# A second norm's scale and shift moved to where a tile is turned, and the last units' way reordered

## The chip, the cores and the metric

The kernel runs on one core of a Trainium2 chip. The metric is the device time of one execution in microseconds. The profile is of one execution, by the hardware profiler. Its engines are TensorE (PE, with its weight loads PEld), VectorE (DVE), ScalarE (ACT), GpSimd (POOL) and SyncE (SP), which issues most DMAs here.

## The reference

Two layers run over x of shape (4, 1024, 256): batch 4, 1024 positions, 256 channels.

```python
x = x + attn(_layernorm(x))          # causal, 16 heads of 16, alibi bias, projection w_proj
x = x + ffn(_layernorm(x))
```

The second one reads its input as T=4, B=1024, C=256, so its own attention is over the four batch rows at each of the 1024 positions, and has then a mixture of experts:

```python
h = _layernorm(x + attn_out, ln1_g, ln1_b)      # scale and shift: gain g, shift b
logits = flat @ router_w.T + router_b           # flat = h.reshape(-1, C)
_, top_i = jax.lax.top_k(softmax(logits), 2)
assign = jnp.max(top_i, axis=-1)                # one expert of 8 for each of 4096 tokens
he = gelu(flat @ w1[e].T + b1[e], approximate=False)
oe = he @ w2[e].T + b2[e]                       # for the assigned expert only
return _layernorm(h + moe_out, ln2_g, ln2_b)    # h is the residual
```

## The kernel before

All work is issued in an order written by the program itself: the kernel's Python simulates the engines' clocks with rough costs and emits each piece where that clock says it is due. What is emitted is fixed; on the chip each engine runs its instructions in that order and waits by semaphores.

**Attention.** Queries are split into units (`units`): a chunk of 256 positions of one batch row; the last chunk's are halves of 128, so that eight small units end the stage. For each unit, TensorE makes scores (tiles `sk`), ScalarE exponentials (`p`), POOL masks the diagonal blocks, TensorE weighs the values (`pv`), and `yt` takes the result. For all but the last unit it goes to DRAM (`y`), comes back in another layout with its sums (`sums`, `yc`), the reciprocals of the sums go out (`r`) and come back broadcast (`su`), VectorE divides (`yc` by `su`), TensorE projects with `wp` (tile `op`) and VectorE adds to x. These are `load_sums`, `invert`, `load_inverse`, `divide` and `projected`, put in due lists by `attended` (L2165), at times after the unit's end named `SUMS_BY`, `INVERTED_BY`, `Y_BY`, `DIVIDED_BY` and `PROJECTED_BY`. The last unit is divided on chip: `normalise` takes sums on TensorE (`sum`), a reciprocal and a product on VectorE (`yn`), and `project_slots` projects it.

**Fronts.** `front(i)` (L1577) does everything of a block of 128 positions x 4 batch rows up to the routing: statistics and root (the root runs on POOL, L814), `u` normalised, turned on TensorE (`utp`, `ut`), products for q, k and v (`qkvp`, copied to `qkv` and `vr`), the small attention over four rows on VectorE (`pr`, `sc`, then `pv`, `ctx`), turned again (`ctp`, `ct`), output product (`ao`), the sum in `u`, the norm (`stats_h`, `rstd_h`), the key, the rank and the one-hot choice (`hot`), then `u` times G1 plus B1, and the place of each token within its expert (`place`). `u` and x (with B2 already added) are stored to DRAM as the two halves of `rows`, through SP's queue. Of the eight fronts, six run beside attention. Fronts 6 and 7 end in the tail; for them ScalarE applies the norms. Each `yield` hands over to the planner, with a kind and a cost.

**Tables and tiles.** Tokens are sorted by expert into tiles of 128. Table 0 has 18 tiles with the tokens of the first six fronts; table 1 has the other 20 and can be made only when front 7's tokens are placed (`who` on TensorE, then some VectorE instructions that end in `rows`, `at_t`, `at_w`). Per tile: POOL gathers the rows (`given`, an indirect DMA, L1849), TensorE turns them (`mtp`), ScalarE copies that (`mt`), TensorE makes `hid` with w1, ScalarE the gelu (`ge`), and TensorE `oe` with w2. The residual is added by a product with the identity (`by_product`: table 0 and the last two tiles), otherwise by VectorE into `given`. Two tiles at a time are finished: statistics, root on POOL (`rstd_v`), two VectorE instructions per tile for the output `o`, and an indirect DMA of POOL that scatters it (L1965), after a small memset (L1964). The queue has 18 buffers for gathered rows and four for `o`.

**The tail** begins after the last attention unit (L2302 on): what is still due, the last unit's division and projection, then a loop that chooses between the steps of fronts 6 and 7, of the tables and of tiles by its own clocks (`free`, `W1_THERE`, `threads[0].ready`).

Of the kernel before, what the change touches and what calls it, by code (L numbers as in the profile page):

```python
# [29 lines left out]
F32 = mybir.dt.float32  # L30
# [7 lines left out]
P = 128  # L38
# [5 lines left out]
CC = C // P  # L44
# [23 lines left out]
HELD_BACK = 5  # L68

TILE = (("PE", 2.6), ("DVE", 1.7), ("ACT", 1.9), ("POOL", 2.3))  # L70
TILE_HALF, LAG, COPIED, FIRST_BY, W1_THERE, LOAD_W2 = 1.3, 0.2, 1.0, 0.1, 22.0, 10.0
KQ_BUFS = 2
D_SLOT = 10.0
SWITCH, COLUMN, EXP_AT_ALL, EXP, READ = 0.2, 1 / 600, 0.17, 1 / 1200, 0.7
AHEAD, EARLY_BY, ROOT, OF_D = 1.0, 0.2, 1.4, 0.35
SUMS_BY, INVERTED_BY, Y_BY, DIVIDED_BY, PROJECTED_BY = 7.0, 14.0, 16.5, 26.0, 28.0

EXP_ZERO = -126 * math.log(2.0)

# [526 lines left out]
def fast_layer(ctx: ExitStack, tc: tile.TileContext, odd, x, wq, wk, wv, wp, w_in, w_out, w_r,  # L606
# [119 lines left out]
    def wide(a):  # L726
        return a.unsqueeze(1).to_broadcast([P, B] + list(a.shape)[1:])
# [130 lines left out]
    def store(key, what):  # L858
        stores.append([key, 0, what])
# [717 lines left out]
    def front(i, fact, more, last):  # L1577
# [14 lines left out]
        def for_later(t):  # L1592

            nc.vector.tensor_tensor(at_x(t), at_x(t), row(B2), ALU.add)
# [21 lines left out]

        yield "D", 2.4
        ut = flipped(u, "ut")
        yield "E", 1.7
        for t in range(B):  # L1620
            for_later(t)
        store(("x", i), store_later)
        yield "DQ" if more else "D", 2.8
        qk = fact.tile([P, B, QC], F32, tag="qkv", name=f"qkv_{i}")
        vr = fact.tile([P, B, C + E], F32, tag="vr", name=f"vr_{i}", bufs=2)
# [74 lines left out]
        if last:  # L1700

            ct = fact.tile(
                [P, CC, QC], F32, tag="turned", name=f"ct_{i}", bufs=TURNED if more else 2
            )

            def turned_sum(t, pr):
                pt = bank(f"ctp_{i}_{t}")[:, :C].rearrange("p (c q) -> p c q", q=P)
                for cc in range(CC):
                    for k in range(B // 2):
                        nc.tensor.matmul(  # L1710
                            pt[:, cc], pr[:, k, cc * P:(cc + 1) * P], ident,
                            start=k == 0, stop=k == B // 2 - 1,
                        )
                nc.scalar.copy(ct[:, :, t * P:(t + 1) * P], pt)

            pr = None
            for t in range(B):
                yield "E", 2.0, 1.0 if t else 0.0
                if t:
                    turned_sum(t - 1, pr)  # L1720
                pr = weighted(t)
                nc.vector.tensor_tensor(pr[:, 0:2], pr[:, 0:2], pr[:, 2:4], ALU.add)
            yield "D", 1.0
            turned_sum(B - 1, pr)
        else:
            ctx_ = fact.tile([P, B, C], F32, tag="ctx", name=f"ctx_{i}")
            for t in range(B):
                yield "E", 2.3
                pr = weighted(t)
                nc.vector.tensor_tensor(pr[:, 0:2], pr[:, 0:2], pr[:, 2:4], ALU.add)  # L1730
                nc.vector.tensor_tensor(ctx_[:, t], pr[:, 0], pr[:, 1], ALU.add)
# [28 lines left out]
        if last:  # L1760
# [4 lines left out]
        norm_apply(  # L1765
            lambda t: u[:, t], lambda t: u[:, t], B, mv, rstd, f"h_{i}", scalar=i >= NT - 2
        )
        key = small.tile([P, B, E], F32, tag="key", name=f"key_{i}", bufs=2)
        best = small.tile([P, B], F32, tag="best", name=f"best_{i}", bufs=2)
        each_e = lambda a: a.unsqueeze(2).to_broadcast([P, B, E])  # L1770
# [27 lines left out]
        nc.vector.tensor_reduce(best, rank, AX.X, ALU.max)  # L1798
        hot = small.tile([P, B, E], BF16, tag="hot", name=f"hot_{i}", bufs=2)
        nc.vector.tensor_tensor(hot, iota, each_e(best), ALU.is_equal)  # L1800
        yield "E", 2.2
        nc.vector.tensor_tensor(u, u, wide(row(G1)), ALU.mult)
        nc.vector.tensor_tensor(u, u, wide(row(B1)), ALU.add)
        store(("u", i), lambda: nc.sync.dma_start(rows_of[:, :, 0:C], u))
        yield ("DC" if last else "D"), 0.8

        if last:
# [31 lines left out]
    class Tile:  # L1839
# [46 lines left out]
        def stages(self):  # L1886


            work, ps, j, name = late["work"], late["ps"], self.j, self.name
            pt = ps.tile([P, CC, P], F32, tag="t", name=f"mtp_{name}")  # L1890
            for cc in range(CC):
                nc.tensor.transpose(pt[:, cc], self.hx[:, cc * P:(cc + 1) * P], ident)
            mt = work.tile([P, CC, P], F32, tag="mt", name=f"mt_{name}")
            nc.scalar.copy(mt, pt)
            if not self.w1:
                self.copy_w1()
            yield
            if not self.w2:
                at = nc.values_load(
                    self.table.at_w[0:1, j:j + 1], engines=[mybir.EngineType.PE],  # L1900
                    min_val=0, max_val=(E - 2) * CC * C,
                    skip_runtime_bounds_check_because="an expert is 1 to E - 1",
                )
            sel = self.table.chosen[:, j:j + 1].to_broadcast([P, P])
            ph = ps.tile([P, CC, P], F32, tag="h", name=f"hid_{name}")
            for fc in range(CC):
                for cc in range(CC):
                    nc.tensor.matmul(
                        ph[:, fc], self.w1[:, cc, fc * P:(fc + 1) * P], mt[:, cc],
                        start=cc == 0, stop=False,  # L1910
                    )
                nc.tensor.matmul(
                    ph[:, fc], b_bf[0][:, fc * P:(fc + 1) * P], sel, start=False, stop=True
                )
            late["n_hid"] += 1
            ge = work.tile([P, CC, P], F32, tag="ge", name=f"ge_{name}")
            nc.scalar.activation(ge, ph, AF.Gelu)
            yield
            if late["n_oe"] % 2 == 0:
                if late["wide"] and late["n_oe"] % 4:  # L1920
                    late["oe"] = bank(f"oe_{name}").rearrange("p (k c) -> p k c", c=C)
                else:
                    late["oe"] = ps.tile([P, 2, C], F32, tag="o", name=f"oe_{name}", bufs=3)
            self.v = late["oe"][:, late["n_oe"] % 2]
            late["n_oe"] += 1
            for fc in range(CC):
                nc.tensor.matmul(
                    self.v, ge[:, fc],
                    self.w2[:, fc] if self.w2 else late["w2"][:, bass.ds(at + fc * C, C)],
                    start=fc == 0, stop=False,  # L1930
                )


            if self.by_product:
                nc.tensor.matmul(self.v, ident, self.hx[:, :C], start=False, stop=False)
            nc.tensor.matmul(self.v, sel, b_bf[1], start=False, stop=True)

    def finish_tiles(two):

        n, name = len(two), two[0].name  # L1940
        for t in two:
            if not t.by_product:
                own = t.hx[:, :C]
                nc.vector.tensor_tensor(own, own, t.v, ALU.add)
                t.v = own
        mv, rstd = norm_stats(lambda k: two[k].v, n, f"v_{name}", "_v")
        norm_root(rstd, n)
        yield
# [26 lines left out]
    class Experts:  # L1975
# [8 lines left out]
        def fetch(self):  # L1984
            self.step += 1
            if tiles_to_do and self.n_fetched - self.n_finished < len(given):
                t = tiles_to_do.pop(0)
                t.by_product = t.table.n == 0 or len(tiles_to_do) < 2
                t.gather(given[self.n_fetched % len(given)])
                if self.n_fetched < N_OWN:  # L1990
                    t.load_weights()
                self.n_fetched += 1
                self.fetched.append((t, self.step))
# [171 lines left out]
    def attended(u, at):  # L2165
        size = units[u][2]
        if u == last_unit:
            return
        for by, what, cost in (
            (SUMS_BY, load_sums, 0.0), (INVERTED_BY, invert, 0.3), (Y_BY, load_inverse, 0.0),  # L2170
            (DIVIDED_BY, divide, 0.5),
        ):
            due_E.append((at + by, cost, lambda what=what: what(u)))
        due_D.append((at + PROJECTED_BY, 0.9 * size, lambda: projected(u)))

    n_projected = [0] * NT

# [111 lines left out]
    for p in range(len(rounds) // 2):  # L2289
# [9 lines left out]
            del waiting[:2]  # L2299
        fill()  # L2300
        E_slot(2 * p + 1, then)
    weigh_next(waiting)  # L2302
    issue_stores(age=0)
    attention.close()
    half_of.clear()
    tail_banks.append(ctx.enter_context(pool("ps_m", 3, space=PSUM)))


    assert not of_E and not of_D, (sorted(of_E), sorted(of_D))
    for _, what in pop_due(due_E + [], 1e9):  # L2310
        what()
    for g in range(2, G):
        normalise(g)
    for _, what in pop_due(due_D + [], 1e9):
        what()
    for it in running:
        it.ready = 0.0
    load_sums(last_unit)
    project_slots()
    tail = ctx.enter_context(pool("tail", 1))  # L2320
    work = ctx.enter_context(pool("work", 2))
    ps_x = ctx.enter_context(pool("ps_x", 1, space=PSUM))
# [46 lines left out]


    threads = [Running(front(NT - 1, fact, 1, True))] + running + [Running(prepare_rest())]
    free = {"PE": 8.0, "DVE": 6.0, "ACT": 2.0, "POOL": 6.0}
    threads[0].ready = 9.0
    engine_of = {"E": "DVE", "P": "DVE", "A": "ACT", "N": "ACT", "R": "POOL", "D": "PE", "d": "PE"}

    def begin(it):
# [149 lines left out]
```

## Time and profile before

| what | value |
|---|---|
| time, median of 3 runs | 809.62 us (807.39 to 810.99) |
| the profiled execution's own time | 812.74 us |
| its span, first to last instruction | 811.0 us |
| granted TensorE clock, mean | 0.958 |
| PE busy | 711.0 us, 88% |
| DVE busy | 544.4 us, 67% |
| ACT busy | 415.7 us, 51% |
| POOL busy | 256.0 us, 32% |
| exponentials of the attention (ACT, `p<-sk`) | 320 instructions, 287.2 us |
| gathers (POOL, L1849) | 38, 42.6 us |
| scatters (POOL, L1965) | 38, 39.7 us |

Busy time is the sum of instructions' durations. An engine can be busy little and yet never rest, since the time between two DMA issues of POOL isn't counted. In the rows of a timeline the columns are start, duration, engine, line, operation, tiles (output before input), shapes and count; the bracket holds the idle time before it and what ended it. Line 587 is the helper that issues every TensorE, VectorE and ScalarE instruction, so these are told apart by their tiles.

### The profile page before, as it was taken

Reading aid. Unit: us, or ns where it says so; the run is one execution under the profiler, and the core shown is the slowest. Engines: PE = TensorE matmul, PEld = TensorE weight load, DVE = VectorE, ACT = ScalarE, POOL = GpSimd, SP = SyncE. Lnnn points to the kernel's source line nnn. Section 1 sums busy time; section 2 is a strip of 40 time slices with the busy share of each in tenths; the row PEclk is TensorE's granted clock in tenths of the full one; section 3 lists DMA queues with packets and bytes.
Section 4 is the critical chain, followed back from the end, with each engine's and each line's share of the span. In section 5 each row is a group of like instructions: output and inputs, shape, how many; then the busy total and the mean of one; then the engine's idle time right before and its main releaser. Section 6 shows DMA issues by size and latency. Waiting matters only on the chain. (4 is left out here: it accounts for less than half of the span.)

```text
span 811.0 us, 22469 instructions
## 1 busy us (share of the span) xinstructions
PE 711.0 (88%) x8917; PEld 534.6 (66%) x8917; DVE 544.4 (67%) x1316; ACT 415.7 (51%) x625; POOL 256.0 (32%) x360
## 2 busy tenths in 40 slices
PE   4989868999999999998999998998995698878882
PEld 3767656666666656575688766787684577667771
DVE  7245325656988675899771538696794589885663
ACT  1454535654656556556657646585573335333440
POOL 5443212221322221113222201131124026648884
PEclk9799989999999999999999999999998699999997
DMA  7344434532354342224545546344433822233430
GB/s 222 110 141 145 143 123 124 159 107 87 86 156 126 108 134 69 91 62 123 152 129 179 151 112 186 110 132 109 147 86 103 289 91 66 79 105 119 127 98 25
DMA packets 75220, 99.56 MB, mean 123 GB/s; under 512 B 19497, under 2 KB 58724, under 8 KB 74597
## 3 DMA queue, kind: packets, MB, share of 16 engines
q1 hardware_dynamic: 62272, 67.84, 28.4%
q10 hardware_dynamic: 7972, 16.05, 6.2%
q0 software_dynamic: 4864, 14.16, 5.9%
q8 instruction: 73, 1.20, 0.7%
q14 instruction: 39, 0.31, 0.1%
HBM read 61.55 MB, written 35.12 MB: 119 GB/s over the span
## 5 line engine op out<-in xcount | busy, mean ns | idle before, releaser
L587 ACT ACTIVATE p<-sk 128x1024 f32<-128x1024 f32 (+1 forms) x320 | 287.2, 940 | 153.4 <-PE sk L587 130.0
L1005 POOL TENSOR_SCALAR_AFFINE_SELECT p<-p 128x512 f32<-128x512 f32 (+1 forms) x160 | 103.5, 651 | 421.9 <-ACT p L587 419.7
L587 PE MATMUL sk<-slots 32*128 32x128 f32 (+1 forms) x3456 | 179.7, 327 | 20.6 <-issue 6.7
L587 PEld LDWEIGHTS sk<-slots 32*128 32x128 f32 x3456 | 137.1, 188 | 64.7 <-issue 32.1
L587 PE MATMUL pv<-p,v 128*32 128x128 f32 (+1 forms) x3456 | 145.9, 315 | 13.6 <-ACT p L587 4.0
L587 PEld LDWEIGHTS pv<-p,v 128*32 128x32 f32 x3456 | 96.7, 111 | 50.1 <-issue 8.4
L587 PE MATMUL qkvp<-w_in,ut 128*128 128x264 f32 (+1 forms) x244 | 85.1, 487 | 0.0
L587 PEld LDWEIGHTS qkvp<-w_in,ut 128*128 128x128 f32 x244 | 43.1, 190 | 29.5 <-issue 24.9
L587 PE MATMUL qkp<-xt,wqk 128*128 128x256 f32 x224 | 56.4, 397 | 0.2 <-ACT p L587 0.2
L587 PE MATMUL oe<-w,ge 128*128 (+1 forms) x152 | 43.1, 408 | 11.7 <-DVE given L587 4.8
L1849 POOL DMA_INDIRECT given<-rows,rows x38 | 42.6, 1122 | 20.9 <-DVE at_t L587 10.0
L587 PEld LDWEIGHTS qkp<-xt,wqk 128*128 128x128 f32 x224 | 41.5, 194 | 11.0 <-issue 3.3
L587 PE MATMUL hid<-mt,w 128*128 128x128 f32 x304 | 46.4, 290 | 2.2 <-ACT ge L587 1.9
L587 PEld LDWEIGHTS hid<-mt,w 128*128 128x128 f32 x304 | 41.3, 197 | 4.0 <-ACT ge L587 2.3
L587 ACT COPY qkv<-qkvp 128x512 f32<-128x512 f32 x29 | 17.0, 585 | 49.9 <-PE qkvp L587 49.8
L1965 POOL DMA_INDIRECT out_dram<-o,out_rows x38 | 39.7, 1044 | 8.7 <-issue 6.1
L587 DVE TENSOR_REDUCE sc<-pr 128x64 f32<-128x1024 f32 x32 | 39.0, 1220 | 1.1
L587 DVE TENSOR_TENSOR pr<-qkv 128x1024 f32<-128x1024 f32 x32 | 39.2, 1224 | 0.2
L587 DVE TENSOR_TENSOR pv<-vr,sc 128x1024 f32<-128x1024 f32 x32 | 39.1, 1222 | 0.2
L587 DVE COPY vr<-qkvp 128x264 f32<-128x264 f32 x28 | 12.1, 432 | 38.0 <-PE qkvp L587 38.0
L587 DVE TENSOR_TENSOR yc<-yc,su 128x512 f32<-128x512 f32 (+1 forms) x19 | 12.3, 647 | 37.6 <-DMA su<-r 37.5
L587 PEld LDWEIGHTS oe<-w,ge 128*128 128x128 f32 x152 | 26.8, 196 | 16.1 <-DVE given L587 6.0
(327 smaller groups left out, 1042.0 us busy)
## 6 DMA issues: line engine op xcount, KB each, us to landing
slots<-k SPq DMA_DIRECT2D x128, 80.0 KB
k<-kq SPq DMA_DIRECT2D x32, 256.0 KB
v<-v ACTq DMA_DIRECT2D x4, 1152.0 KB
x<-in_x_dram SPq DMA_DIRECT2D x16, 256.0 KB
y<-yt SPq DMA_DIRECT2D x16, 256.0 KB
rows<-x SPq DMA_DIRECT2D x32, 128.0 KB
slots<-k SPq DMA_DIRECT2D x64, 64.0 KB
rows<-u SPq DMA_DIRECT2D x8, 512.0 KB
```

What stands on the lines that cost most here:

```text
L587: ins = made(*args, **kwargs)
L1005: nc.gpsimd.affine_select(blocks, blocks, pattern=[[0, 2], [0, size], [1, P]], compare_op=ALU.is_ge, fill=0.0, base=0, channel_multiplier=-1,)
L1849: nc.gpsimd.indirect_dma_start(out=self.hx, out_offset=None, in_=t.rows_of, in_offset=bass.IndirectOffsetOnAxis(ap=t.rows_[:, self.j:self. ...
L1965: ins = nc.gpsimd.indirect_dma_start(out=out.rearrange("t n c -> (t n) c"), out_offset=bass.IndirectOffsetOnAxis(ap=t.table.out_rows[:, t. ...
```

## The change

It has two parts.

*Scale and shift.* `u` is stored as it comes from the norm; the two VectorE instructions with G1 and B1 are gone, and the store is asked for directly after the norm. Where a tile is turned, ScalarE applies gain and shift while copying out of PSUM: in turned form a channel is a partition, so both are one value per partition (`columns`). That takes one instruction for each half of the channels, and four buffers for `mt` instead of two, since `mt` is read again later: the residual is now a product of the turned tile with the identity, for every tile, which turns it back. The sum in `oe` now starts with the bias, then the residual, then w2. The VectorE add of the residual is gone.

*Order.* For the last unit but one the loads and the inverse are due sooner, its division and projection only after the last unit's own. The remaining due work comes in another order. In front 7, B2 is added to x and stored later, after the attention over the rows. The planner's constants for the tail are changed, and the front's step of 2.2 that held the two removed instructions is gone, so that what follows it is placed differently everywhere, on all engines.

```diff
-TILE_HALF, LAG, COPIED, FIRST_BY, W1_THERE, LOAD_W2 = 1.3, 0.2, 1.0, 0.1, 22.0, 10.0
+TILE_HALF, LAG, COPIED, FIRST_BY, W1_THERE, LOAD_W2 = 1.3, 0.2, 1.0, 0.1, 14.0, 2.0
+NEVER, HURRIED = 1e6, {SUMS_BY: 2.0, INVERTED_BY: 5.5, Y_BY: 7.5}
...
         ut = flipped(u, "ut")
-        yield "E", 1.7
-        for t in range(B):
-            for_later(t)
-        store(("x", i), store_later)
+        if not last:
+            yield "E", 1.7
+            for t in range(B):
+                for_later(t)
+            store(("x", i), store_later)
...
             turned_sum(B - 1, pr)
+            for t in range(B):
+                for_later(t)
+            store(("x", i), store_later)
...
+        store(("u", i), lambda: nc.sync.dma_start(rows_of[:, :, 0:C], u))
...
-        yield "E", 2.2
-        nc.vector.tensor_tensor(u, u, wide(row(G1)), ALU.mult)
-        nc.vector.tensor_tensor(u, u, wide(row(B1)), ALU.add)
-        store(("u", i), lambda: nc.sync.dma_start(rows_of[:, :, 0:C], u))
...
-            mt = work.tile([P, CC, P], F32, tag="mt", name=f"mt_{name}")
-            nc.scalar.copy(mt, pt)
+            mt = work.tile([P, CC, P], F32, tag="mt", name=f"mt_{name}", bufs=4)
+            for cc in range(CC):
+                nc.scalar.activation(
+                    mt[:, cc], pt[:, cc], AF.Identity,
+                    bias=columns[:, 1, cc:cc + 1], scale=columns[:, 0, cc:cc + 1],
+                )
...
+            nc.tensor.matmul(self.v, sel, b_bf[1], start=True, stop=False)
+            for cc in range(CC):
+                nc.tensor.matmul(
+                    self.v[:, cc * P:(cc + 1) * P], mt[:, cc], ident, start=False, stop=False
+                )
...
-            if self.by_product:
-                nc.tensor.matmul(self.v, ident, self.hx[:, :C], start=False, stop=False)
-            nc.tensor.matmul(self.v, sel, b_bf[1], start=False, stop=True)
...
-        for t in two:
-            if not t.by_product:
-                own = t.hx[:, :C]
-                nc.vector.tensor_tensor(own, own, t.v, ALU.add)
-                t.v = own
...
+            if u == last_unit - 1:
+                by = HURRIED.get(by, NEVER)
             due_E.append((at + by, cost, lambda what=what: what(u)))
-        due_D.append((at + PROJECTED_BY, 0.9 * size, lambda: projected(u)))
+        by = NEVER if u == last_unit - 1 else PROJECTED_BY
+        due_D.append((at + by, 0.9 * size, lambda: projected(u)))
...
+    for _, what in pop_due(due_E, NEVER):
+        what()
     weigh_next(waiting)
-    issue_stores(age=0)
...
-    for _, what in pop_due(due_E + [], 1e9):
-        what()
+
+    take_E()
     for g in range(2, G):
         normalise(g)
-    for _, what in pop_due(due_D + [], 1e9):
+        busy("DVE", 1.3)
+    project_slots()
+    for _, what in pop_due(due_E, 2 * NEVER) + pop_due(due_D, 2 * NEVER):
         what()
+    issue_stores(age=0)
+    load_sums(last_unit)
     for it in running:
         it.ready = 0.0
-    load_sums(last_unit)
-    project_slots()
...
-    free = {"PE": 8.0, "DVE": 6.0, "ACT": 2.0, "POOL": 6.0}
-    threads[0].ready = 9.0
+    free = {"PE": 0.0, "DVE": 0.0, "ACT": 0.0, "POOL": 0.0}
+    threads[0].ready = 0.0
```

More of the change, by code (lines that the diff above doesn't have):

```diff
@@ L1929, in stages @@
                     self.w2[:, fc] if self.w2 else late["w2"][:, bass.ds(at + fc * C, C)],
-                    start=fc == 0, stop=False,
+                    start=False, stop=fc == CC - 1,
                 )
-            if self.by_product:
-                nc.tensor.matmul(self.v, ident, self.hx[:, :C], start=False, stop=False)
-            nc.tensor.matmul(self.v, sel, b_bf[1], start=False, stop=True)
     def finish_tiles(two):
         n, name = len(two), two[0].name
-        for t in two:
-            if not t.by_product:
-                own = t.hx[:, :C]
-                nc.vector.tensor_tensor(own, own, t.v, ALU.add)
-                t.v = own
         mv, rstd = norm_stats(lambda k: two[k].v, n, f"v_{name}", "_v")
@@ L1987, in fetch @@
                 t = tiles_to_do.pop(0)
-                t.by_product = t.table.n == 0 or len(tiles_to_do) < 2
                 t.gather(given[self.n_fetched % len(given)])
```

## The prediction

> **What bounds the kernel now.** I read the page's 40 slices first. Each slice is 20.3 us and each digit is a tenth.
>
> ```profile
> PE   4989868999999999998999998998995698878882
> DVE  7245325656988675899771538696794589885663
> POOL 5443212221322221113222201131124026648884
> PEclk9799989999999999999999999999998699999997
> ```
>
> There are two regimes. Up to slice 30 (about 617 us) the attention keeps TensorE at nine tenths. From 150 to 617 us TensorE is busy for 446.3 of 467 us, and of the waits named there only 4.7 us in all are on VectorE. Work taken from VectorE there is worth little. After 617 us (the tail) TensorE is patchy and POOL rises to eight tenths. So I read the tail in stretches of 20 us.
>
> ```profile
> core 0: us, PE busy (x) PEld busy (x) DVE busy (x) ACT busy (x) POOL busy (x), PEclk, DMA share, GB/s
> ...
> 720.00:740.00 20.00, 13.12 (x68) 10.91 (x67) 12.03 (x36) 4.81 (x11) 17.06 (x24) 0.83 0.42 125
> 740.00:760.00 20.00, 18.35 (x132) 16.05 (x130) 13.76 (x42) 9.69 (x23) 16.65 (x24) 1.00 0.44 134
> 760.00:780.00 20.00, 17.34 (x122) 14.95 (x122) 11.97 (x37) 9.41 (x22) 17.01 (x23) 1.00 0.42 118
> 780.00:800.00 20.00, 13.96 (x95) 11.76 (x93) 13.98 (x42) 5.18 (x12) 15.70 (x27) 1.00 0.21 64
> ```
>
> POOL shows 16 to 17 of 20 us although it never rests, as its timeline tells:
>
> ```profile
> 719.56 1.01 POOL L1849 DMA_INDIRECT given<-rows,rows  x1 [10.00 <-DVE at_t L587]
> ...
> 766.67 1.05 POOL L1849 DMA_INDIRECT given<-rows,rows  x1 [0.30 <-issue]
> 767.75 0.73 POOL L814 TENSOR_TENSOR rstd_v<-rstd_v,minus_half 128x2 f32<-128x2 f32 x1
> 768.66 1.28 POOL L1849 DMA_INDIRECT given<-rows,rows  x1 [0.19 <-issue]
> 769.95 0.12 POOL L1964 MEMSET spare<- 128x1 f32 x1
> 770.25 1.02 POOL L1965 DMA_INDIRECT out_dram<-o,out_rows  x1 [0.18 <-issue]
> ```
>
> Two tiles (two gathers, one root, two scatters) take from 766.67 to 772.88, so 6.2 us, 3.1 a tile. Between instructions there are only issue gaps of 0.2 to 0.3. TensorE needs 2.3 us a tile there. **From 719.56 to its last scatter at 803.91 the kernel is bound by POOL**, and 7.1 us of landing and end follow. 719.56 is when the second table is known. Before it POOL had waited 10.0 us. So the end is set by two things: when the second table's first gather starts (T), and how much POOL work is then left (84.35 us now, for 20 gathers and 32 of 38 scatters).
>
> T hangs on the last block, front 7, and that on the end of attention:
>
> ```profile
> DVE yc L587 <- DMA su<-r: 9.5, 1, 9.5
> ...
> PE op L587 <- DVE yc L587: 3.7, 1, 3.7
> ```
>
> The load of the inverse sums (su) is issued at 624.33 on SP's queue, behind a store of y that waits for ScalarE (623.88), though its source was stored at 618.8.
>
> **Scale and shift (VectorE, ScalarE, TensorE).** Removed: two VectorE instructions per front and 18 residual adds (0.42 each).
>
> ```profile
> 708.96 2.48 DVE L587 TENSOR_TENSOR u<-u,rows 128x1024 f32<-128x1024 f32 x2
> ...
> 661.09 0.59 PE L587 MATMUL oe<-given,ident 128*128 128x256 f32 x2
> ```
>
> Six fronts' 2.48 us (14.9 in all) lie in attention, beside a full TensorE. Bounds there are -4.7 (every VectorE wait goes) and +5 (fronts now meet other slots, in whose queues a ScalarE copy can stand before an exponential). I take -1. Front 7's 2.48 is on the path. In the other direction, the product with the identity starts 0.43 after its predecessor (661.09 to 661.52). The turned tile needs two products of 128 columns, and the nearest row, hid from mt, takes 0.45 for two. So the 18 tiles of table 0 and the last two cost the same, and 18 tiles gain 0.43, making 2.74 us: +7.8 us of TensorE, still under POOL's 3.1, so nothing. If POOL were out of the way, all 7.8 would count. ScalarE's copy (0.37) becomes two instructions of 128x128. No row shows that form. The copy of yt, 128x128, is 0.26, so 0.52; four ACTIVATEs of 128x256 take 2.08, so at most 1.04 for two. I take 0.52, +0.15 a tile, hidden by the 1.0 to 1.5 us of oe that stands between mtp and its hid. At 1.04 it would start to show only where TensorE is ahead of nothing. Without the adds a tile's PSUM is held until its output is made. With three banks more in this part (12 tiles in all) that is cover enough.
>
> **The last units.** I read beside the trace the order in which the changed kernel's instructions stand on each engine (it holds no times). In it su is loaded before both stores of y. Price: the reciprocal of the sums moves ahead of a full VectorE queue (0.25, or 0.5 if the sums land late), behind which TensorE's last products wait. I add 0.5. Then, by rows of before:
> - yt copied 624.4; its sums 625.6; two reciprocals and products (2 x 1.28) 627.6; the last quarter of the 3.52 us slot product 628.5; add 629.0, yc 629.4, product with wp 2.08 to 631.5, add: x complete at 632.0 (now 634.64).
> - pv and ctx of front 6 (2.3) and four small ones now stand in the stall, so front 7's statistics start at 632.0 (now 637.67) and the root is back at 636.3. But the shift is queued behind front 6's first two adds of ao: ctp to 633.5, ct 635.0, two ao 2.97 to 638.0, shift 638.6, ScalarE's four 2.08, turning and copies 1.4: front 7's first qkv product at 642.2 (now 650.69, where all four ao stood before it).
> - The fourth qkv waits behind `place`, which waits for front 6's hot: ao 640.0, adds and statistics 642.7, root 644.0, key to hot 4.66, so 648.7; qkv copied 651.4. First pr at 651.4 (now 659.59).
> - Four pr/sc and the maximum, 11.0 with nothing between: 662.4 (now 676.08; u's 2.48, table work 2.1 and tile statistics stood between). Exponential, sums, four pv and one pair's statistics, 11.0: 673.4 (now 691.54, with two pairs' outputs and statistics, 3.1 each, between).
> - ctp, ao and statistics 6.6: 680.0; root 1.2, no longer covered; key 2.3, one pair 3.2, hot 2.2, one pair 3.2: 692.1; table 8.2 as now (711.36 to 719.56): 700.3.
> - Late next: POOL's queue now has a root (rstd_v_6) before the first gather, and its statistics stand on VectorE behind the table's last row (701.7): +1.3, +0.9: 704.0.
>
> **A rule against this.** Tiles leave front 7's stretch, so TensorE idles there. The row: after 3.06 us of idle (to 623.90) the granted clock is 0.50 until 632; after a gap of 2.1 us (702.3) oe takes 2.02 for 1.08. The Trainium skill ("TensorE: Matmul & The Clock Gate", section "Why this matters for your kernels") says that TensorE should not idle over about 3 us between bursts, or it falls back to half rate. If the gaps count as such, front 7's ctp and ao (5.3) double, +5.3. By the row of front 7 before, gaps of 0.7 to 1.3 between ctp (686 to 692) kept ao at full clock, 0. The new gaps are 1 to 2 us: I take +1, T = 705.0, **14.6 us earlier**.
>
> **What POOL takes back.** At T the changed order has 34 scatters left instead of 32 and one root more: 2 x 1.31 + 0.92 = 3.5. And its next root waits until 707.5 for statistics queued behind the pair o_4, o_5 (idle 1.3); the next outputs wait for scatters to land (another 1.2). Together 6.0.
>
> **Sum.** -14.6 + 6.0 - 1 = -9.6 on the span, so 801.4 for 811.0. The profiled execution took 812.74, 1.74 around the span, so it would take 803.1. The median shown is 3.1 below that execution: **800**.
>
> **Rivals.**
> - *POOL gives nothing back* (its idle is filled by the extra scatters, no clock loss): -15.6 - 1, 793. For: 18 gathers fit before T. Against: outputs 4 to 7 stand on VectorE behind the table. 0.14.
> - *The table is hardly earlier*: seven tiles stand before `place` on TensorE, and at clock 0.5 from 662 on these and ctp/ao (7 x 2.74 = 19 us, and 5.3) would cost up to 24; from about 10 the gain is gone: 810. For: the clock rows above. Against: VectorE, not TensorE, is last there by 2 us. 0.11.
> - *Slower: attention pays.* One place: ScalarE's queue in six fronts. A ct, ut or qkv copy that waits for its product stands before exponentials; TensorE then waits as it does for yt now (4.0 us, two waits, longest 3.1). At 3.1 per front and two copies each that is up to 37; from 2.3 per front (14) the whole is slower by 4, 814. Against: the same copies stand before exponentials now, at 3.5 us of waits in all for ten pv. 0.13.
>
> The forecast has 0.62. About 0.5% (4 us) is what a measurement can tell from no change. The forecast's own range is 795 to 806; the range to 792 and 809 takes in most of the first two rivals. Faster by over 0.5%: the forecast, the first rival and little else, 0.75; within: 0.13; slower: 0.12.
>
> **What would show it.** First gather of table 1 near 705 and last scatter near 794, POOL without rest between them; yc not waiting for su; x complete near 632, first pr near 651, four pr without gaps; oe at 7 instructions in every tile and 2.74 us; mt twice 0.26. Wrong if the end of attention moves by over 3 us from 617, if granted clock from 660 to 690 falls under 0.8, or if POOL idles over 5 us after its first gather.

## The result and the profile after

The changed kernel takes 803.39 us (median of 10 runs, 801.24 to 805.99). The kernel before, run beside it 10 times, takes 810.59 us (807.39 to 814.89). The ratio is 0.9902, with a 95% interval of 0.9878 to 0.9926: faster by about 1%. The profiled execution took 802.74 us, with a span of 801.0 (812.74 and 811.0 before). The forecast was 800 us and a span of 801.4. All ratios here leave out executions over 1.5% above the fastest of the same kernel; the profile of e10 below is of such an execution.

The slices of the changed kernel, 20.0 us each:

```profile
PE   4889869999998999999889999899998687979993
DVE  7245324747887574889672338588689788865553
POOL 5443202312222120114221211123112230788874
PEclk9799979999999999999999999999999999999997
```

VectorE's 31st and 32nd digits are 9 and 7 where they were 4 and 5: it is the engine that front 7 hangs on, and it rests less at the begin of the tail. POOL's 7s and 8s begin at the 35th digit, where 6 and 4 stood before the 8s, and its total is nearly the same (254.1 us for 256.0). In the granted clock the 8 and 6 of the 31st and 32nd are gone.

The stretches of 20 us in which the second table's tiles run (busy time and count of each engine, then granted clock):

```profile
core 0: us, PE busy (x) PEld busy (x) DVE busy (x) ACT busy (x) POOL busy (x), PEclk, DMA share, GB/s
720.00:740.00 20.00, 18.31 (x143) 16.94 (x141) 11.62 (x33) 11.98 (x27) 17.27 (x23) 1.00 0.42 126
740.00:760.00 20.00, 18.88 (x146) 17.41 (x145) 10.12 (x29) 12.58 (x28) 17.13 (x23) 1.00 0.43 127
760.00:780.00 20.00, 18.75 (x146) 17.26 (x145) 11.72 (x35) 12.06 (x27) 15.14 (x25) 1.00 0.30 90
780.00:800.00 20.00, 7.18 (x52) 6.28 (x50) 7.23 (x22) 1.58 (x4) 10.78 (x18) 0.77 0.09 26
```

Up to 760 POOL has the same 17 of 20 us as before, but TensorE now has 18 to 19 where it had 17 to 18. Two engines are near their limit, not one. POOL's timeline, with the first gather of table 1 in its fourth row and the first wait of over half a microsecond behind it in its last:

```profile
701.49 1.02 POOL L1967 DMA_INDIRECT out_dram<-o,out_rows  x1 [0.19 <-issue]
...
702.81 1.00 POOL L1967 DMA_INDIRECT out_dram<-o,out_rows  x1 [0.19 <-issue]
703.83 0.92 POOL L815 TENSOR_TENSOR rstd_v<-rstd_v,minus_half 128x2 f32<-128x2 f32 x1
704.95 1.07 POOL L1852 DMA_INDIRECT given<-rows,rows  x1 [0.20 <-issue]
...
774.05 0.71 POOL L815 TENSOR_TENSOR rstd_v<-rstd_v,minus_half 128x2 f32<-128x2 f32 x1 [1.33 <-DVE rstd_v L588]
```

So T, the start of the second table's first gather, is 704.95 (before 719.56). The row that makes the second table's gathers possible is this one of VectorE:

```profile
700.28 0.18 DVE L588 TENSOR_SCALAR at_t<-block 128x20 int32<-128x20 int32 x1
```

It ends 4.5 us before T. In the kernel before, the first gather had waited for that row and came at once. Here POOL has had only the gaps between issues since 687.14, and works off a gather, two scatters and a root first. So in the changed kernel it is POOL's own queue that sets T in the end, no longer the table.

Two tiles still take 6.2 us of POOL until about 770; then POOL waits twice for statistics (1.33 and 1.37 us), which wait for TensorE. From T to the end of the last scatter (793.82) it is 88.87 us (84.35 before). In the list of VectorE's waits from 612 to 645, the one of 9.5 us for `su` is gone:

```profile
DVE x L588 <- PE op L588: 3.0, 2, 2.2
DVE u L588 <- PE ao L588: 1.6, 3, 0.6
```

One tile's `oe` on TensorE and the two instructions for `mt` (76 of them, mean 455 ns):

```profile
743.45 0.27 PE L588 MATMUL oe<-b_bf,chosen 128*128 128x256 bf16 x1
743.56 0.61 PE L588 MATMUL oe<-ident,mt 128*128 128x128 f32 x4
744.01 1.03 PE L588 MATMUL oe<-w,ge 128*128 x4
```
```profile
L588 ACT ACTIVATE mt<-mtp,columns 128x128 f32<-128x128 f32 x76 | 30.7, 455 | 30.6 <-PE mtp L588 30.6
```

The products with w2 start 0.45 us later for the residual's four. Where TensorE doesn't wait, gelus follow one another by 2.70 us, which is its time for a tile.

### The profile page after: what moved, and what is told of

It reads as the page before. It is cut to its first block, busy times and chain, and to the rows that moved or that the text cites. A ratio compares the mean times of both kernels' runs of the same rounds, so it can differ in the third digit from the quotient of the medians.

```text
span 801.0 us, 22678 instructions
## 1 busy us (share of the span) xinstructions
PE 710.5 (89%) x9029; PEld 538.2 (67%) x9029; DVE 521.5 (65%) x1282; ACT 433.0 (54%) x663; POOL 254.1 (32%) x360
## 4 chain that ended last, share of the span: by engine, by line
PE 53%; DVE 20%; DMA 8%; issue 7%; POOL 6%; ACT 3%; SPq 1%; ACTq 0%; POOLq 0%; DVEq 0%
PE sk L588 14%; PE pv L588 11%; PE qkvp L588 9%; PE qkp L588 6%; PE vp L588 5%; DVE pv L588 4%; POOL given L1852 3%; ACT p L588 2%; PE oe L588 2%; DVE sc L588 2%; PE op L588 2%; DVE pr L588 1%; PE ao L588 1%; DVE u L588 1%; DMA out_dram<-o,out_rows 1%
## 5 line engine op out<-in xcount | busy, mean ns | idle before, releaser
L1006 POOL TENSOR_SCALAR_AFFINE_SELECT p<-p 128x512 f32<-128x512 f32 (+1 forms) x160 | 105.6, 664 | 426.9 <-ACT p L588 424.9
L588 PE MATMUL pv<-p,v 128*32 128x128 f32 (+1 forms) x3456 | 143.4, 313 | 10.3 <-ACT p L588 4.0
L588 ACT ACTIVATE mt<-mtp,columns 128x128 f32<-128x128 f32 x76 | 30.7, 455 | 30.6 <-PE mtp L588 30.6
L588 DVE COPY kq<-qkp 128x512 f32<-128x512 f32 x28 | 19.1, 683 | 43.1 <-PE qkp L588 42.7
L588 PE MATMUL hid<-mt,w 128*128 128x128 f32 x304 | 44.6, 283 | 2.6 <-ACT ge L588 1.7
L588 PE MATMUL oe<-w,ge 128*128 (+1 forms) x152 | 40.0, 386 | 0.0
## 6 DMA issues: line engine op xcount, KB each, us to landing
k<-kq SPq DMA_DIRECT2D x32, 256.0 KB
x<-in_x_dram SPq DMA_DIRECT2D x16, 256.0 KB
y<-yt SPq DMA_DIRECT2D x16, 256.0 KB
```

The costliest lines, as they stand in the source:

```text
L588: ins = made(*args, **kwargs)
L1006: nc.gpsimd.affine_select(blocks, blocks, pattern=[[0, 2], [0, size], [1, P]], compare_op=ALU.is_ge, fill=0.0, base=0, channel_multiplier=-1,)
```

## The experiments

Executions begin unevenly: the first `yt` copy comes between 35.0 and 38.7 us. In this table all marks of a profiled execution are therefore counted from its first `yt` copy. "Last exp" is the attention's last exponential, "x" the begin of front 7's statistics (its x is complete), "pairs" the pairs of tiles whose outputs VectorE makes between x and front 7's `hot`, "after T" the time from T to the end of the last scatter. The ratio is to the kernel before, run on the same chip in the same session; the sessions differ, so ratios less than 0.003 apart are not told apart. Each row's marks are of one execution.

| kernel | last exp | x | T | x to T | pairs | after T | ratio (95%) |
|---|---|---|---|---|---|---|---|
| before | 577.7 | 600.1 | 682.0 | 81.9 | 4 | 84.4 | 1 |
| changed | 579.4 | 595.0 | 666.9 | 71.9 | 1 | 88.9 | 0.9902 (0.9878 to 0.9926) |
| e1 scale and shift alone | 584.6 | 603.9 | 682.8 | 78.8 | 3 | 85.2 | 1.0006 (0.9974 to 1.0039) |
| e8 the same, step kept | 577.7 | 597.2 | 675.7 | 78.5 | 4 | 85.4 | 0.9964 (0.9944 to 0.9983) |
| e2 order alone | 578.0 | 592.4 | 670.5 | 78.0 | 1 | 89.4 | 0.9926 (0.9902 to 0.9950) |
| e3 changed, step kept | 580.4 | 594.8 | 670.0 | 75.2 | 1 | 89.2 | 0.9938 (0.9908 to 0.9968) |
| e5 old planner constants | 578.9 | 596.0 | 666.2 | 70.1 | 1 | 88.3 | 0.9889 (0.9836 to 0.9942) |
| e6 old way of the last units | 582.9 | 599.8 | 686.0 | 86.2 | 4 | 84.9 | 1.0066 (1.0042 to 1.0090) |
| e11 e6 with one call | 583.0 | 604.6 | 676.2 | 71.6 | 1 | 89.9 | 1.0009 (0.9984 to 1.0034) |
| e7 B2 added early | 579.6 | 595.6 | 668.2 | 72.6 | 2 | 93.1 | 0.9950 (0.9926 to 0.9974) |

**Which half of the change brings the gain (e1, e2, e8, e3).** e1 is the kernel before with the scale-and-shift part, e2 the changed kernel without it.

> The kernel before with the scale-and-shift part alone; order and the planner's constants of the tail are as before. Theory (the time follows the start T of the second table's first gather, POOL-bound after it): front 7's two VectorE instructions (2.48 us) leave T's path and little else, so T about 717 for 719.6 and a time of about 808 us, ratio to before 0.995 to 1.000. Rival (VectorE's relief is the gain): at least 5 us faster, ratio under 0.994. Third (attention pays, as the changed kernel's 2.1 us later last exponential suggests): last exponential near 617.4 instead of 615.3 and a ratio of 1.000 to 1.003.

> The changed kernel with the scale-and-shift part undone: u times G1 plus B1 by VectorE in its own step of 2.2, one copy for mt, residual by a product of the gathered rows or by VectorE. Theory: front 7's 2.48 us come back on T's path, so T about 707.5 and a time of about 806 us, ratio to before 0.993 to 0.996. Rival (scale and shift is the gain): ratio 0.998 or more. If the removed step's changed placement is what moved the end of attention by 2.1 us, the last exponential is back near 615.3 here, and the ratio can reach 0.991.

The order alone gives 0.9926, which is not told apart from the whole change (0.9902). Scale and shift alone gives nothing in e1: x to T is 3.1 us shorter, where u's 2.48 us stood, but the last exponential comes 6.9 us later. The list of TensorE's waits in the attention from 300 us on (total, times, longest) has, in e1, these two rows that the kernel before lacks (it has one of `sk` on `yt` instead, 3.1 us):

```profile
PE place L587 <- DVE hot L587: 3.0, 2, 2.7
...
PE sk L587 <- DVE kq L587: 2.1, 1, 2.1
```

The removed step of 2.2 in the planner had stood between `hot` and `place`. Without it TensorE is told to place a block at once and stands there until VectorE has the choice, scores behind it. These rows don't add up to 6.9 us. The changed kernel has the same two rows (3.0 and 2.1 us) and its last exponential at 579.4, so they can't be the whole cause. e8 keeps an empty step:

```diff
+        yield "E", 2.2
         yield ("DC" if last else "D"), 0.8
```

> The kernel before with the scale-and-shift part, but an empty step of cost 2.2 kept in the front where the two instructions stood. In the run of that part without the step the last exponential came 6.9 us later than before (counted from the first yt copy), while place on TensorE waited for hot for 3.6 us, and the tail was 6.1 us shorter, so nothing was left. If the missing step's placement is what attention pays for: the last exponential within 3 us of before's, T 3 to 5 us earlier than before's, ratio 0.994 to 0.997. If the loss is of another cause: last exponential again 5 us or more later, ratio 1.000.

The wait is gone, the last exponential is back at 577.7, and the ratio is 0.9964 (its interval and e1's just overlap). T is 6.3 us earlier than before: 3.4 from x to T, and 2.9 before x, where a wait of `yt` that only the profile of before shows is missing (below).

> The changed kernel with an empty step of cost 2.2 left in the front where the two removed instructions stood, so that the planner places what follows it as before. If the placement moved the end of attention, the last exponential is at about 615.3 instead of 617.4, T near 703, and the time 801 to 802 us, ratio to before 0.988. If not, 617.4 and the changed kernel's 803.4, ratio 0.990.

In the changed kernel the same step brings nothing: the wait of `place` is gone, an old one of `sk` on `yt` (3.1 us) is back, and the ratio is 0.9938, whose interval overlaps the changed kernel's. And the last exponential of one execution cannot be read so finely. All ten kernels without the step (changed, e1, e4 to e7, e9 to e12) have VectorE's work of attention in one order up to the last units, and all ten have the two rows of waits. Their last exponential comes at 578.2 to 585.0, the latest in e10. So e1's 584.6 is within what executions of one order differ by. The four kernels with a step (before, e2, e3, e8) have it at 577.7 to 580.4. TensorE's waits for `hot`, `kq` and `yt` come to 2.4 us more in e1 than in e8 (3.0, 2.1 and 0.4 us for one of 3.1), and to as much more in the changed kernel than in e3. That the missing step costs attention some 2 us is likely by this; the ratios don't show it.

**Which piece of the order (e5, e6, e7, e11).** e5 has the old constants, e6 the old due times and the old sequence after the last unit, e7 adds B2 in front 7 at the old place:

```diff
-TILE_HALF, LAG, COPIED, FIRST_BY, W1_THERE, LOAD_W2 = 1.3, 0.2, 1.0, 0.1, 14.0, 2.0
+TILE_HALF, LAG, COPIED, FIRST_BY, W1_THERE, LOAD_W2 = 1.3, 0.2, 1.0, 0.1, 22.0, 10.0
...
-    free = {"PE": 0.0, "DVE": 0.0, "ACT": 0.0, "POOL": 0.0}
-    threads[0].ready = 0.0
+    free = {"PE": 8.0, "DVE": 6.0, "ACT": 2.0, "POOL": 6.0}
+    threads[0].ready = 9.0
```
```diff
-            if u == last_unit - 1:
-                by = HURRIED.get(by, NEVER)
...
-    take_E()
+    for _, what in pop_due(due_E + [], 1e9):
+        what()
     for g in range(2, G):
         normalise(g)
...
-    project_slots()
...
+    load_sums(last_unit)
+    project_slots()
```
```diff
-        if not last:
-            yield "E", 1.7
...
+        yield "E", 1.7
...
```

> The changed kernel with the planner's constants of the tail as before (W1_THERE 22, LOAD_W2 10, the engines' start clocks 8/6/2/6, the front's 9). T is counted from the first yt copy, since executions begin up to 3.7 us apart: 667.0 in the changed kernel, 682.0 before. If the constants are what keeps tiles' work out of front 7's stretches (some 9 us of VectorE work stood there before), T comes back by 5 to 9 us, with up to 2 us of it given back by scatters that are then done before T: ratio to before 0.994 to 1.000. If the constants do nothing by themselves: T within 1 us, ratio 0.990.

> The changed kernel with the last two units' way as before: due times of the last unit but one, and the order of what is left after the last unit. If the hurried load of the inverse sums is what matters: front 7's x is complete some 2 us later and its statistics stand some 4 us later, T later by 3 to 5 us, ratio 0.994 to 0.996. If VectorE's other work fills that wait: T within 1 us, ratio 0.990.

> The changed kernel with front 7's B2 added to x, and x stored, at the place before (after turning u). Theory: the four adds (1.7 us of VectorE) stand where VectorE waits for the q, k, v products anyway: T within 0.5 us and ratio 0.990. If they delay front 6's last steps and with them place and the fourth qkv: T later by 1.7 us, ratio 0.992.

The constants do nothing measurable. e6 loses the whole gain and more. A stretch of VectorE in e6 shows where, between front 7's last product for the maximum and the step after it:

```profile
668.79 1.22 DVE L588 TENSOR_REDUCE sc<-pr 128x64 f32<-128x1024 f32 x1
669.93 0.47 DVE L588 SCALAR_TENSOR_TENSOR o<-oe,mv_v,rows 128x256 f32<-128x256 f32 x1
670.50 0.48 DVE L588 SCALAR_TENSOR_TENSOR o<-o,rstd_v,given 128x256 f32<-128x256 f32 x1
...
673.11 0.58 DVE L588 TENSOR_REDUCE top<-sc 128x64 f32<-128x256 f32 x1
...
689.14 0.19 DVE L588 TENSOR_TENSOR hot<-low_con,expert 128x32 bf16<-128x32 f32 x1
```

A pair of tiles takes its 3.2 us on VectorE in the middle of front 7's chain, and the `hot` at 689.14 is front 6's: front 6 is finished only after front 7's maximum, and the planner sees front 7 late and fills with tiles. In the changed kernel front 6's `hot` stands 13.2 us ahead of that maximum. The written order of instructions says which line does this: not a due time but the one call `take_E()` after the last weighing, which issues what the fronts can issue there. e11 is e6 with that line:

```diff
     for _, what in pop_due(due_E + [], 1e9):
         what()
+    take_E()
     for g in range(2, G):
```

> The changed kernel with the last two units' way as before (as the run that was slower than before by 0.7%), but with the one planner call kept that issues what fronts can issue right after the last unit's weighing. By the written order alone, that call puts front 6's last VectorE steps ahead of front 7's and leaves one pair of tiles' outputs between front 7's maximum and its hot, where there are three without it and one more between x and the maximum. If that placement is the gain: x to T is 72 to 76 us (86.2 without the call, 71.9 in the changed kernel), T within 4 us of the changed kernel's 666.9 counted from the first yt copy, ratio 0.990 to 0.995. If the hurried load of the inverse sums is the gain: T stays later by over 10 us and the ratio at 1.000 or more.

Half of the first expectation holds, and the other half falls. x to T is 71.6 us, the changed kernel's 71.9: the one call is worth 14.6 us there. But x itself comes 9.5 us after the changed kernel's. 3.6 of these are in attention, no more than executions of one order differ by; in the rest VectorE again waits for the late load of the inverse sums, and front 6's products, which the call has put there, stand behind that wait:

```profile
621.87 0.24 DVE L588 RECIPROCAL inverse<-sums 128x16 f32<-128x16 f32 x1
629.88 0.43 DVE L588 TENSOR_TENSOR yc<-yc,su 128x256 f32<-128x256 f32 x1 [7.77 <-DMA su<-r]
630.23 1.22 DVE L588 TENSOR_TENSOR pv<-vr,sc 128x1024 f32<-128x1024 f32 x1
```

With the call and none of the rest the kernel takes as long as before (1.0009). That is 0.0057 better than e6, but not the gain. So the call keeps tiles out of front 7's chain, and the rest, the hurried load with the last unit's own division first, lets the chain begin in time. (This rest was not run without the call, and the hurried load and the sequence of the divisions were not tried apart.)

In e7 x to T is only 0.7 us longer and the pairs between x and `hot` are two, but the ratio is 0.9950. In its profile the loss is behind T: 93.1 us for 88.9. There POOL waits 3.7 us for statistics at 709.97, and 2.4 us for an output near the end, and doesn't make them good. (Another wait of 4.3 us ends at T itself.)

**What binds after T (e4, e9, e10, e12).** e4 leaves out the memset ahead of each scatter, e9 POOL's root for the tiles, e10 adds one product per tile (zeros, 256 columns):

```diff
-            nc.gpsimd.memset(spare, 0.0)
```
```diff
-        norm_root(rstd, n)
```
```diff
+            nc.tensor.matmul(self.v, ident, nothing.to_broadcast([P, C]), start=False, stop=False)
```

> The changed kernel without the small memset of POOL ahead of each scatter (0.12 us and the 0.2 us gap to the next issue, 38 times, 34 of them after T). If POOL alone bounds after T: 34 times 0.3 is 10 us less, about 793 us, ratio to before 0.979. If TensorE is right behind (18.3 to 18.9 us busy of 20 in the changed kernel): one pair falls from 6.2 to some 5.9 us, 3 to 5 us in all, about 799 us, ratio 0.985. If the time of the memset is only moved into the scatter's own issue (its wait now stands on the DMA): no change, ratio 0.990.

> The changed kernel without POOL's root for the tiles' last norm: the outputs are scaled by the variance plus epsilon instead of by its inverse root. That takes 0.92 us (0.74 and the gap) per two tiles from POOL, about 17 times after T. If POOL alone sets the pace there: two tiles fall from 6.22 to 5.30 us, 15 us in all, last scatter some 73 us after T, ratio to before 0.971. If TensorE is right behind it (18.3 to 18.9 us busy of 20): two tiles at 5.8 to 6.0 us, 4 to 7 us in all, ratio 0.982 to 0.986. If POOL doesn't set it: ratio 0.990.

> The changed kernel with one more product of 256 columns per tile, of the identity with zeros (0.43 us of TensorE a tile, as the residual product of before). If POOL has room over TensorE after T: two tiles stay at 6.22 us and the ratio at 0.990 to 0.992 (some of it before T). If TensorE is as full as POOL: two tiles go to 6.4 to 6.9 us, 3 to 12 us more, ratio 0.994 to 1.005.

e4: 0.9917 (0.9887 to 0.9947), after T 89.9 us: no change. The time is not freed, it becomes a longer gap to the next issue:

```profile
743.12 1.28 POOL L1852 DMA_INDIRECT given<-rows,rows  x1 [0.19 <-issue]
744.71 1.02 POOL L1966 DMA_INDIRECT out_dram<-o,out_rows  x1 [0.30 <-issue]
746.03 1.00 POOL L1966 DMA_INDIRECT out_dram<-o,out_rows  x1 [0.30 <-DVE rstd_v L588]
```

e9: 0.9832 (0.9758 to 0.9906; four executions, and the interval just includes the changed kernel's ratio). Two tiles fall from 6.2 to 5.39 us on POOL, twice TensorE's 2.70, but after T only 1.6 us are won (87.3 for 88.9); another 4.5 us lie before T, where roots stood ahead of the first gathers. The second table is known at the same time in both, 662.0 us after the first `yt` copy for 662.3. But without roots POOL's queue is empty then, and its first gather follows at once (the profile puts the end of that last wait down to TensorE):

```profile
698.51 0.18 DVE L588 TENSOR_SCALAR at_t<-block 128x20 int32<-128x20 int32 x1
698.86 1.04 POOL L1852 DMA_INDIRECT given<-rows,rows  x1 [1.55 <-PE hid L588]
```

From 740 to 780 of e9 TensorE never rests:

```profile
740.00:760.00 20.00, 20.00 (x159) 18.68 (x158) 11.87 (x34) 13.26 (x30) 16.34 (x24) 1.00 0.51 138
760.00:780.00 20.00, 20.00 (x158) 18.76 (x157) 11.79 (x35) 11.20 (x26) 7.67 (x14) 1.00 0.14 48
```

e10: 1.0020 (0.9993 to 1.0047), so about 10 us were added by 0.43 us a tile. Of the 17.0 us by which its profiled execution is longer than the changed kernel's, 7.4 lie after T, 5.2 from x to T, and 4.3 before x, where no tile runs yet. The gelus of its last 15 tiles or so follow one another by 3.13 us instead of 2.70, and now POOL waits for statistics, as it did for at most 1.4 us in the changed kernel:

```profile
792.77 0.38 ACT L588 ACTIVATE ge<-hid 128x256 f32<-128x256 f32 x1 [0.31 <-PE hid L588]
795.90 0.38 ACT L588 ACTIVATE ge<-hid 128x256 f32<-128x256 f32 x1 [0.31 <-PE hid L588]
```
```profile
795.51 0.72 POOL L815 TENSOR_TENSOR rstd_v<-rstd_v,minus_half 128x2 f32<-128x2 f32 x1 [2.83 <-DVE rstd_v L588]
```

The traces of the two together show it: when POOL becomes faster, TensorE is the limit at 2.70 us a tile, and when TensorE becomes slower, it is the limit at once. In the changed kernel 26 of 38 gelus come after T, so TensorE needs 26 x 2.70 = 70.2 us, of 79.5 from T to the last gelu.

e12 tries to use this, with the root on VectorE after the second table (an integer guess and two Newton steps, eight small instructions of about 0.2 us):

> The changed kernel with the root of the tiles' last norm on VectorE after the second table is known: an integer guess and two Newton steps, eight instructions on 128x2 in place of one of POOL. POOL loses 0.92 us per two tiles, VectorE gains about 8 times 0.2 = 1.7 us (10.1 to 11.7 us of 20 now, so up to 17). Without the root TensorE's 2.70 us a tile set the pace. If VectorE has that room: 2 to 6 us less, ratio 0.983 to 0.988. If the eight instructions delay statistics or outputs in VectorE's queue, so that TensorE's banks come free later: ratio 0.990 or above.

0.9910 (0.9877 to 0.9943): no gain. POOL's pair falls to 5.3 to 5.4 us again and VectorE has room (15 to 17 of 20 us busy), but from T to the last scatter it is 90.2 us. TensorE's waits from 700 to 780 have this row in e12, and then in the changed kernel:

```profile
PE oe L588 <- DVE stats_v L588: 7.3, 3, 5.1
```
```profile
PE oe L588 <- DVE stats_v L588: 8.7, 7, 3.1
```

The longest of these is at the same place in both: TensorE's next `oe` has no free bank of PSUM until VectorE, busy with the second table's last rows and then with outputs, has read an earlier one. In e12 the eight instructions of the root stand in that queue too, and the wait is 5.1 us for 3.1. Behind it TensorE runs at 2.70 us a tile, and from T to the last gelu both kernels take as long (79.4 and 79.5 us). What follows the last gelu has become longer (10.8 us for 9.4), with POOL waiting up to 3.0 us for each pair's outputs. No version tried is clearly faster than the changed kernel: e9 leaves out a part of the result, and its interval and e5's include the changed kernel's ratio.

## Why the prediction was right, and where it was not

- **T and POOL's work after it as what sets the end: right.** The legs agree within 0.6 us: front 7's first q, k, v product 642.2 (641.68), first `pr` 651.4 (651.71), maximum 662.4 (662.80), end of `pv` 673.4 (673.77), rank 692.1 (692.27), table 700.3 (700.46). T was put at 705.0 and is 704.95.
- **Part of this nearness is luck.** The last exponential came 2.1 us later than before, and the way from it to the last `yt` copy was 2.2 us shorter, since a wait of 7.16 us that only the profile of before shows is missing. So the legs began at the right moment for a reason that the forecast didn't have:

```profile
615.25 1.02 ACT L587 ACTIVATE p<-sk 128x1024 f32<-128x1024 f32 x1 [0.16 <-PE pv L587]
...
623.59 0.27 ACT L587 COPY yt<-pv 128x128 f32<-128x128 f32 x1 [7.16 <-remote]
```
```profile
617.39 1.03 ACT L588 ACTIVATE p<-sk 128x1024 f32<-128x1024 f32 x1 [0.15 <-PE pv L588]
...
623.49 0.27 ACT L588 COPY yt<-pv 128x128 f32<-128x128 f32 x1 [4.92 <-PE pv L588]
```

- **The last step to T: right about the place, less so about the wait.** The forecast has the root ahead of the first gather wait for statistics, and adds 1 us for the clock, which was not needed. The statistics were there at 703.19; the root then stood 0.6 us longer behind POOL's own two scatters. e3 shows how much play there is: its table is known 7.5 us later than the changed kernel's, counted from the first `yt` copy, and its T is only 3.1 us later.
- **The span within 0.4 us: two misses that cancel.** The forecast took 1 us off for attention besides T, so its T was 704.0 in effect, 1.0 too early; and POOL took back 4.5 us (88.87 less 84.35), not 6.0. The two scatters and the root that the order adds are there, at 3.5 as reckoned; of the 2.5 us of waits only 1 came.
- **"+7.8 us of TensorE, still under POOL's 3.1, so nothing": right in the sum, by a narrow margin.** The tile costs 2.70 us (2.74 forecast). But the comparison of 2.74 with 3.1, time for a tile, left out how much each engine still has to do at T: 26 tiles for TensorE, 70.2 of the 79.5 us. e10 shows that another 0.43 us would have cost all of the gain.
- **PSUM as "cover enough": right.** TensorE's `oe` waits for a bank in both kernels. From 700 to 800 it waits 8.7 us in all in the changed kernel (the row above, no other of `oe`), and 11.7 before, partly for the residual adds that are gone:

```profile
PE oe L587 <- DVE given L587: 4.8, 5, 1.4
PE oe L587 <- DVE stats_v L587: 3.7, 1, 3.7
PE oe L587 <- DVE mv_v L587: 3.2, 1, 3.2
```

- **The last units: right in kind.** VectorE no longer waits for `su`, and x is complete at 633.2 (632.0 forecast), with front 6's `pv` ahead of the last division. The reciprocal of the sums cost 1.0 us rather than 0.5. What the forecast read off the written order without naming its cause, front 7's chain almost free of tiles, e6 and e11 put down to one call.
- **Attention -1: not borne out.** The pair of profiles has +1.7, and ten executions of one order spread over 6.8. The third rival has something real in it, though: without the step TensorE waits some 2.4 us more in attention, in e1 and in the changed kernel alike. The place is not ScalarE's queue, as the rival had it, but `place` and `kq`, for which TensorE waits on VectorE.
- **`mt` 0.52: it is 0.80 for two** (two instructions of 0.455, overlapping), within the bounds, and hidden: from 700 to 800 TensorE has no wait for `mt`.
- **The clock rule: rightly not followed for front 7's stretch.** The granted clock is 1.00 from 640 to 700 with gaps of up to 1.74 us on TensorE there. A longer gap does show it, behind T: after 3.15 us of waiting the four products of `oe` with w2 take 1.90 us for 1.03 elsewhere, and the granted clock from 700 to 720 is 0.91.

```profile
706.00 0.37 PE L588 MATMUL oe<-b_bf,chosen 128*128 128x256 bf16 x1 [3.15 <-DVE stats_v L588]
706.17 1.06 PE L588 MATMUL oe<-ident,mt 128*128 128x128 f32 x4
707.02 1.90 PE L588 MATMUL oe<-w,ge 128*128 x4
```

- **The number: 3.4 us too low, by its last term.** The step to the median took 3.1 us off, because the profiled execution of before lay that much above three runs. Against ten runs it lay 2.15 above, and the changed kernel's profiled execution lies 0.65 below its own median. An offset of one execution from a median says nothing of the next one.

## What to carry to other kernels

Where a program plans its own order, removing an instruction also removes its slot, and what stood behind it can run into a wait that the slot had covered: keep the slot as an experiment before blaming the instruction. A chain that sets the end is shortened most by what is kept out of it, and that can leave the whole time as it was (e11) while the chain's input still comes late. Once a chain is shorter, look again at what the last step waits for: here it is no longer the table but POOL's queue. Before calling added work hidden under the slowest engine, compare the total that each engine still has to do in that stretch, not the time per piece.

## What the runs showed of the hardware

- A small POOL instruction between two indirect DMA issues was free here (e4). With the memset the row is 1.02 us of scatter, 0.12 of memset, 0.18 to 0.19 of gap; without it 1.02 and a gap of 0.30.
- The first `yt` comes at 35.0 to 38.7 us in fourteen profiled executions, though VectorE and ScalarE have the same instructions in the same order up to there in all of them. In the ten with one order in attention, its length from there to the last exponential is 578.2 to 585.0 us, in steps of 1 to 4 us that are partly made good later. A single profile cannot tell differences of this size.
- ScalarE applies gain and shift to a 128x128 half out of PSUM in 0.455 us, two in 0.80, where one plain copy of 128x256 took 0.37 (before).
- A wait of 7.16 us that ends in "remote", ahead of the last `yt` copy, is in the profile of before only; from the last exponential to that copy it is 8.3 us there, and 5.1 to 7.2 in all others, e1, e8 and e2 among them. What it waited for was not found.
